# Four images' q*v products and Toeplitz products issued between the parts of the first image's front, and q*v in blocks of 128 tokens

## The chip, the cores and the metric

One core of a Trainium2 chip runs the whole program. The metric is the time of one execution on the device in microseconds; three executions of the kernel before are given. The core has a matrix engine (TensorE, PE in the profile, with PEld for its weight loads), a vector engine (VectorE, DVE), a scalar engine (ScalarE, ACT), GpSimd (POOL) and a sync engine (SyncE, SP), which in this kernel does little but issue DMAs. Each engine works through its own queue of instructions in order.

## The reference, cut to what matters

Eight images of 56 x 56 tokens with 192 channels pass through four layers, each added to its input and each preceded by a group norm: a gated Toeplitz layer, a shifted-window attention, a depthwise 3x3 convolution and a selective scan. The change concerns the first layer:

```
q, v, p = silu(gn(x) @ q_w.T + q_b), silu(... v_w ...), silu(... p_w ...)   # 192 -> 576 channels
qv = q * v
o1 = toeplitz(qv along w, a1)      # 576 channels, a 56 x 56 Toeplitz matrix per channel
o2 = toeplitz(qv along h, a2)
x  = x + (p * (o1 + o2)) @ o_w.T + o_b
```

The Toeplitz coefficients a1 and a2 come from a small network and a decay and are the same for all images. The other three layers follow image by image; the scan of layer 3 runs in four directions over 3136 tokens with 384 channels of 16 states each. All arithmetic is float32.

## The kernel before, in words

The program has five parts, in this order.

**Coefficients** (lines 145 to 184): both tables of Toeplitz coefficients are computed and put into DRAM (`ext`).

**q*v products** (lines 187 to 221): for each of the eight images, x is loaded on SP's queue, its group statistics are taken, and x is normalized. Then 28 blocks of TT = 112 tokens are multiplied with the 1152 columns of the q and v weights in three column groups of 384, each as two matmuls (lines 213 and 214, the two halves of the channels). ScalarE applies Silu (line 215), VectorE multiplies q with v (line 216), and the result is stored on SP's queue (line 218) to `qv_d`. A float32 matmul stands in the trace as two records, so 8 x 28 x 3 x 2 = 1344 matmuls are some 2688 records.

**Toeplitz products** (lines 224 to 277): for each of two axes, for each of six blocks of 96 channels (`c0`), both groups of four images are loaded as `tzx` (line 250, 16 DMAs on SP's queue, one for each image and half, 56 partitions each; along h the pieces in DRAM are 28 x 96 contiguous floats, along w they are 96 floats, 384 bytes). Within a block there are four groups of 24 channels: two DMAs on SP's queue (line 258) spread the coefficients of a group into one of three `tm` tiles of 112 x 24 x 112, as two diagonal 56 x 56 Toeplitz blocks, in runs of 224 bytes. Each channel and each group of four images is one 112 x 112 x 112 matmul (line 263). ScalarE and VectorE take turns (line 269) in copying four channels' result back into `tzx`, and 16 DMAs on GpSimd's queue (line 277) store the block. A `tm` load must wait until TensorE is done with the tile's previous contents, three groups earlier. A `tzx` load must wait for the store of the block that had the buffer before.

**Set-up and front of image 0**: constants, the attention's bias and masks (98 tiny DMAs on ScalarE's queue, line 339), the convolutions' diagonal matrices, and then `front(0)` (line 1133), which is the part of all four layers ahead of the scans: `gate` (416), `attention` (495), `conv2` (676), `inner` (757) and `steps` (833). They are generators that yield between pieces of work. Their instructions have line 76 in the trace for image 0, since they pass through a recorder (`Meter`) whose costs the later planner uses. `front(0)` is run to its end by `drain`, with nothing between its pieces.

**Scans** (from line 1137): a written order, with a planner that steps the front of the next image and the end of the last one into the gaps of the scans. The planner's costs come from the record of `front(0)`.

Outside the scans the framework places the instructions of each engine by its own schedule, with the program's order as priority; the order that comes out is known from the built program. The two Toeplitz steps and the front share the in-order queue of SP for their loads, and the pools of SBUF and PSUM decide what has to wait for what.

Of the kernel before, what the change touches and what calls it, by code (L numbers as in the profile page):

```python
# [15 lines left out]
F32 = mybir.dt.float32  # L16
AF = mybir.ActivationFunctionType
# [5 lines left out]
H = W = 56  # L23
# [58 lines left out]
def model(ctx: ExitStack, tc: tile.TileContext, a: dict, out: bass.AP):  # L82
# [5 lines left out]
    def load_const(pool, name, eng=None):  # L88
        t = pool.tile(list(a[name].shape), F32, name=name + "_sb")
        (eng or nc.sync).dma_start(out=t, in_=a[name])  # L90
        return t
# [24 lines left out]
    def blocks(ap):  # L116
        return ap.rearrange("(k p) l -> p k l", p=CP)

    def group_stats(x, sp, ps, mean_out, rstd_out):

        st = sp.tile([CP, 2, NCH, 6], F32, name="gn_st")
        mv = sp.tile([CP, 2, 2], F32, name="gn_mv")
        for k in range(2):
            for j in range(NCH):
                nc.vector.bn_stats(out=st[:, k, j, :], in_=x[:, k, j * CH : (j + 1) * CH])
            nc.vector.bn_aggr(out=mv[:, k, :], in_=st[:, k].rearrange("p j s -> p (j s)"))
        pm = ps.tile([128, 512], F32, name="ps_gn", tag="ps")
        nc.tensor.matmul(pm[:CP, 0:2], gmat, mv[:, :, 0], start=True, stop=True)
        nc.vector.tensor_copy(mean_out, pm[:CP, 0:2])

        dm = sp.tile([CP, 2], F32, name="gn_dm")
        nc.vector.tensor_sub(dm, mv[:, :, 0], mean_out)
        nc.vector.tensor_mul(dm, dm, dm)
        nc.vector.tensor_add(dm, dm, mv[:, :, 1])
        pv = ps.tile([128, 512], F32, name="ps_gn", tag="ps")
        nc.tensor.matmul(pv[:CP, 0:2], gmat, dm, start=True, stop=True)
        sd = sp.tile([CP, 2], F32, name="gn_sd")
        nc.scalar.activation(sd, pv[:CP, 0:2], AF.Sqrt, bias=eps5[:CP])
        nc.vector.reciprocal(rstd_out, sd)

    def normalize(dst, src, mean, rstd):
        nc.vector.tensor_scalar(dst, src, mean, rstd, ALU.subtract, ALU.mult)
# [41 lines left out]
            nc.gpsimd.dma_start(out=blocks(ext[i]), in_=ea)  # L184


    with (
        tc.tile_pool(name="qv_w", bufs=1) as wp,
        tc.tile_pool(name="qv", bufs=2) as sp,
        tc.tile_pool(name="qv_ps", bufs=2, space=PSUM) as ps,  # L190
        tc.tile_pool(name="qv_ps4", bufs=6, space=PSUM) as ps4,
    ):
        wqv = wp.tile([CP + 1, 2, 2 * D1], F32, name="wqv")
        nc.sync.dma_start(out=wqv[:CP, 0, :], in_=a["wqv"][0:CP])
        nc.sync.dma_start(out=wqv[:, 1, :], in_=a["wqv"][CP : 2 * CP + 1])
        for b in range(B):
            x = sp.tile([CP, 2, L], F32, name="x0")
            nc.sync.dma_start(out=x, in_=blocks(a["x"][b]))
            group_stats(x, sp, ps, stats0[:, b, :, 0], stats0[:, b, :, 1])
            xn = sp.tile([CP + 1, 2, L], F32, name="xn0")  # L200
            nc.gpsimd.memset(xn[CP : CP + 1, 1, :], 1.0)

            for k in range(2):
                normalize(xn[:CP, k, ::-1], x[:, k], stats0[:, b, k, 0:1], stats0[:, b, k, 1:2])
            for g in range(NCH):
                qv = sp.tile([TT, 4, D1], F32, name="qv")
                for t in range(4):
                    tok = slice((4 * g + t) * TT, (4 * g + t + 1) * TT)
                    sl = sp.tile([TT, 2 * D1], F32, name="sl", bufs=3)
                    for n in range(3):  # L210
                        pq = ps4.tile([TT, 384], F32, name="ps_qv")
                        col = slice(n * 384, (n + 1) * 384)
                        nc.tensor.matmul(pq, xn[:CP, 0, tok], wqv[:CP, 0, col], start=True, stop=False)
                        nc.tensor.matmul(pq, xn[:, 1, tok], wqv[:, 1, col], start=False, stop=True)
                        nc.scalar.activation(sl[:, col], pq, AF.Silu)
                    nc.vector.tensor_mul(qv[:, t, :], sl[:, :D1], sl[:, D1:])
                for c in range(D1 // CP):
                    nc.sync.dma_start(
                        out=qv_d[b][c, g * CH : (g + 1) * CH, :].rearrange("(t p) c -> p t c", p=TT),
                        in_=qv[:, :, c * CP : (c + 1) * CP],  # L220
                    )


    NB = min(4, B)
    TC = 24
    G = NB * (H // 2)
    with (
        tc.tile_pool(name="tz", bufs=4) as sp,
        tc.tile_pool(name="tz_t", bufs=1) as tp,
        tc.tile_pool(name="tz_ps", bufs=8, space=PSUM) as ps,  # L230
    ):

        tm = [tp.tile([TT, TC, TT], F32, name=f"tm{i}") for i in range(3)]
        for t in tm:
            nc.gpsimd.memset(t, 0.0)
        n_t = 0
        for ax in range(2):
            along_h = "(h u w) c -> u h w c"
            along_w = "(u h w) c -> u w h c"
            stored = "(w u h) c -> u w h c"  # L240
            size = dict(h=H, u=2) if ax == 0 else dict(w=W, u=2)
            for c0 in range(D1 // CP):
                xs = []
                for b0 in range(0, B, NB):
                    x = sp.tile([TT, G, CP], F32, name="tzx")
                    xs.append((b0, x))
                    for b in range(NB):
                        v = qv_d[b0 + b][c0].rearrange(along_w if ax else along_h, **size)
                        for u in range(2):
                            nc.sync.dma_start(out=x[u * W : (u + 1) * W, b * 28 : (b + 1) * 28, :], in_=v[u])  # L250
                for c1 in range(0, CP, TC):
                    t = tm[n_t % 3]
                    n_t += 1
                    e = ext[1 - ax][c0 * CP + c1 : c0 * CP + c1 + TC, :]

                    src = bass.AP(e.tensor, e.offset, [[1, W], [TT, TC], [1, W]])
                    for u in range(2):
                        nc.sync.dma_start(out=t[u * W : (u + 1) * W, :, u * W : (u + 1) * W], in_=src)
                    for b0, x in xs:
                        for c2 in range(0, TC, 4):  # L260
                            po = ps.tile([TT, 4, G], F32, name="ps_tz")
                            for c in range(4):
                                nc.tensor.matmul(  # L263
                                    po[:, c, :], t[:, c2 + c, :], x[:, :, c1 + c2 + c], start=True, stop=True
                                )
                            cs = slice(c1 + c2, c1 + c2 + 4)
                            copy = nc.vector.tensor_copy if (c2 // 4) % 2 else nc.scalar.copy

                            copy(  # L269
                                x[:, :, cs].rearrange("p (b g) c -> p b g c", b=NB)[:, :, ::-1, :],  # L270
                                po.rearrange("p c (b g) -> p b g c", b=NB),
                            )
                for b0, x in xs:
                    for b in range(NB):
                        v = o_d[ax][b0 + b][c0].rearrange(stored if ax else along_h, **size)
                        for u in range(2):
                            nc.gpsimd.dma_start(out=v[1 - u], in_=x[u * W : (u + 1) * W, b * 28 : (b + 1) * 28, :])  # L277


    with (  # L280
        tc.tile_pool(name="w", bufs=1) as wp,
        tc.tile_pool(name="sc", bufs=2) as sp,
        tc.tile_pool(name="bc", bufs=NP) as bcp,
    ):
        p_b, o_b, qkv_b, pr_b = (load_const(wp, n) for n in ("p_b", "o_b", "qkv_b", "pr_b"))
        cb2, cb3, dt_b = (load_const(wp, n) for n in ("cb2", "cb3", "dt_b"))
        ln_g, ln_b, w_out, w_dt = (load_const(wp, n) for n in ("ln_g", "ln_b", "w_out", "w_dt"))
# [5 lines left out]
        nc.vector.memset(ones, 1.0 / DI)  # L293
        zero2 = wp.tile([128, NG], F32, name="zero2")
        nc.vector.memset(zero2, 0.0)

        ysum = wp.tile([128, ND, L], F32, name="ysum")
        slab = wp.tile([128, SLAB], F32, name="slab")
        slab_f = wp.tile([128, SLAB_F], F32, name="slab_f")

# [651 lines left out]
        pairs = [(i, d, k) for i in range(len(chunks)) for d in range(ND) for k in range(NP)]  # L952
        bms, cms, deltas, dus, xcs, states, hss, das, hcs, yps, xds = ({} for _ in range(11))

        delta2 = wp.tile([128, 2, ND, CH + 2], F32, name="delta2")

        for u in range(2):
            nc.gpsimd.memset(delta2[:, u, :, 0 : CH + 2 : CH + 1], 1e30)

        def load_bc(i, k):  # L960
            b, slot, j = chunks[i]
            for ts, name, r0 in ((bms, "bm", 0), (cms, "cm", NS)):
# [166 lines left out]
                pass  # L1129


        with tc.tile_pool(name="ps0", bufs=8, space=PSUM) as ps:
            drain(front(0), costs.setdefault("front", []))
        psa = ctx.enter_context(tc.tile_pool(name="ps_a", bufs=2, space=PSUM))
        psy = ctx.enter_context(tc.tile_pool(name="ps_y", bufs=2, space=PSUM))
        ps = ctx.enter_context(tc.tile_pool(name="ps", bufs=2, space=PSUM))
# [196 lines left out]
```

## Time and profile before

| what | value |
|---|---|
| median of three executions | 22507.34 us (22483.73 to 22516.53) |
| the profiled execution | 22523.93 us |
| its span | 22522.1 us |
| TensorE busy | 18316.9 us (81%) |
| VectorE busy | 16557.5 us (74%) |
| GpSimd busy | 16170.0 us (72%) |
| ScalarE busy | 12501.5 us (56%) |
| first scan (line 1017) starts | 3738.0 us |

The page divides the span into 40 slices of 563 us each and gives the busy share of each engine in tenths. Line numbers are those of the kernel before. A group such as "L263 PE MATMUL ps_tz<-tzx,tm" is a line, an engine, an operation and the tiles that it writes and reads. What follows "idle before" or stands in square brackets is the time for which the engine stood still ahead of the instruction and what released it; "issue" means that the profile shows no releaser. SPq rows are DMAs being issued on SP; their second column is the time that the issuing took, with what it had to wait for in its queue.

### The profile page before, as it was taken

To read this page: it belongs to the slowest core of one execution; us is meant where nothing else is said; L and a number is where in the kernel's file an instruction comes from. 1 tells how busy PE (TensorE), PEld (TensorE's weight loads), DVE (VectorE), ACT (ScalarE), POOL (GpSimd) and SP (SyncE) were. 2 spreads that over 40 slices of the span, in tenths; PEclk is the share of its full clock that TensorE was granted. 3 is DMA by queue.
4 is the path that set the end of the run, shared out by engine and by line. 5 is a ranking of instruction groups with operands and counts; after the bars stand their busy time and mean duration, and the time that the engine had idled before them with its cause. 6 is when DMAs were issued, how large, how long until landed. Compare 5 with 4: busy or idle time off the path is not lost. (4 is left out here: it accounts for less than half of the span.)

```text
span 22522.1 us, 201129 instructions
## 1 busy us (share of the span) xinstructions
PE 18316.9 (81%) x58660; PEld 9648.2 (43%) x58660; DVE 16557.5 (74%) x13156; ACT 12501.5 (56%) x31864; POOL 16170.0 (72%) x8500
## 2 busy tenths in 40 slices
PE   8866677878897888888887888788978888887666
PEld 4566433434343344434443444344434444343233
DVE  3211113997699868997799779986898789967998
ACT  3311234665667566655666576746665666556555
POOL 0000003897789878887898778977898789878999
PEclk9988778989899999999999989998999999998888
DMA  3479215444553456445544455345534564445333
GB/s 90 106 197 187 74 47 160 140 131 147 176 155 124 135 172 176 122 128 166 180 132 127 156 183 148 120 141 179 167 118 133 163 187 130 123 149 179 129 129 110
DMA packets 2536340, 3220.45 MB, mean 143 GB/s; under 512 B 1045261, under 2 KB 2488687, under 8 KB 2504272
## 3 DMA queue, kind: packets, MB, share of 16 engines
q1 hardware_dynamic: 2515010, 3091.32, 46.2%
q0 software_dynamic: 15520, 116.14, 1.3%
q8 instruction: 465, 7.62, 0.1%
q14 instruction: 641, 5.25, 0.1%
q10 hardware_dynamic: 4704, 0.12, 0.0%
HBM read 2631.56 MB, written 575.48 MB: 142 GB/s over the span
## 5 line engine op out<-in xcount | busy, mean ns | idle before, releaser
L993 POOL TENSOR_TENSOR hs<-du,bm 128x896 f32<-128x896 f32 x5376 | 11140.7, 2107 | 87.2 <-DVE ps_a L1017 46.9
L1038 PE MATMUL ps_y<-hc,ident_sb 128*128 128x448 f32 x21504 | 9845.4, 592 | 742.9 <-POOL hc L1023 665.7
L1017 DVE TENSOR_TENSOR_SCAN ps_a<-ps_a,hs 128x898 f32<-128x898 f32 x3360 | 6796.3, 2023 | 1093.1 <-ACT ps_a L1008 895.4
L1008 ACT ACTIVATE ps_a<-delta,A_logs_sb 128x449 f32<-128x449 f32 x10752 | 6859.9, 638 | 355.0 <-DVE hs L1017 72.9
L1038 PEld LDWEIGHTS ps_y<-hc,ident_sb 128*128 128x128 f32 x21504 | 4290.3, 208 | 4809.5 <-issue 3546.5
L1023 POOL TENSOR_TENSOR hc<-hs,cm 128x896 f32<-128x896 f32 x2016 | 4077.0, 2022 | 2194.0 <-DVE hs L1017 1054.5
L1023 DVE TENSOR_TENSOR hc<-ps_a,cm 128x896 f32<-128x896 f32 x3360 | 3667.7, 1092 | 1207.7 <-PE ps_y L1038 921.5
L1017 DVE TENSOR_TENSOR_SCAN hs<-ps_a,hs 128x898 f32<-128x898 f32 x2016 | 4063.4, 2016 | 331.2 <-ACT ps_a L1008 253.6
L1030 ACT COPY state<-ps_a 128x2 f32<-128x2 f32 x3359 | 528.9, 157 | 3950.3 <-DVE hc L1023 3947.8
L981 POOL TENSOR_TENSOR du<-delta,xcd 128x448 f32<-128x448 f32 x672 | 719.6, 1071 | 1268.7 <-DMA xcd<-xc 1268.7
L263 PE MATMUL ps_tz<-tzx,tm 112*112 112x112 f32 x4608 | 889.5, 369 | 471.4 <-issue 272.2
L277 POOL DMA_DIRECT2D o<-tzx x192 | 97.9, 514 | 1498.7 <-DVE tzx L269 1018.6
L803 PE MATMUL ps_f<-slab 128*128 128x448 f32 x2646 | 1090.3, 548 | 60.1 <-DMA slab<-dg_d 48.0
L263 PEld LDWEIGHTS ps_tz<-tzx,tm 112*112 112x112 f32 x4608 | 884.0, 200 | 477.1 <-issue 476.0
L269 DVE COPY tzx<-ps_tz 112x448 f32<-112x448 f32 x288 | 179.9, 624 | 1180.3 <-PE ps_tz L263 910.5
L269 ACT COPY tzx<-ps_tz 112x448 f32<-112x448 f32 x288 | 153.3, 532 | 1206.0 <-PE ps_tz L263 975.2
L998 ACT COPY hs<-state 128x2 f32<-128x2 f32 x4608 | 817.5, 177 | 2.7 <-POOL hc L1023 2.5
L76 PE MATMUL ps_f<-slab 96*96 96x448 f32 (+6 forms) x2306 | 744.8, 519 | 87.7 <-DMA slab<-x 35.5
L633 PE MATMUL ps_f<-ident_sb,slab 98*98 98x98 f32 x1344 | 331.7, 315 | 586.2 <-ACT slab L626 586.2
L735 PE MATMUL ps_f<-slab 96*96 96x448 f32 x1764 | 725.5, 547 | 40.8 <-DVE slab L722 40.8
L803 PEld LDWEIGHTS ps_f<-slab 128*128 128x128 f32 x2646 | 507.7, 193 | 560.7 <-issue 502.5
L1030 ACT COPY state<-hs 128x2 f32<-128x2 f32 x2016 | 379.0, 188 | 581.5 <-DVE hs L1017 545.1
(215 smaller groups left out, 17752.8 us busy)
## 6 DMA issues: line engine op xcount, KB each, us to landing
bm<-bc SPq DMA_DIRECT2D x1792, 448.0 KB
cm<-bc SPq DMA_DIRECT2D x1792, 448.0 KB
xcd<-xc SPq DMA_DIRECT2D x840, 224.0 KB
dl<-slab SPq DMA_DIRECT2D x224, 672.0 KB
delta<-dl SPq DMA_DIRECT2D x224, 672.0 KB
tzx<-qv SPq DMA_DIRECT2D x192, 588.0 KB
o<-tzx POOLq DMA_DIRECT2D x192, 588.0 KB, 16.5
slab<-x SPq DMA_DIRECT2D x224, 336.0 KB
```

Source lines behind the costliest of these rows:

```text
L76: return f(*args, **kw)
L263: nc.tensor.matmul(po[:, c, :], t[:, c2 + c, :], x[:, :, c1 + c2 + c], start=True, stop=True)
L735: nc.tensor.matmul(p[:CP, :CH], dg[:, k, t, :], xp[:, u, k, dy : dy + 8, dx : dx + W], start=t == 0, stop=t == 8,)
L803: nc.tensor.matmul(p[:, :CH], dg[:, t, :], xp[:, 8 * j + dy : 8 * j + dy + 8, dx : dx + W], start=t == 0, stop=t == 8,)
L981: nc.gpsimd.tensor_mul(du[:, 0, :], deltas[i][:, d, 1 : CH + 1], xcs.pop((i, d)))
L993: nc.gpsimd.tensor_mul(hs[:, :, tokens(i)[0]], dus[i, d].to_broadcast([128, NG, CH]), bms[i, k])
L998: nc.scalar.copy(hss[g][:, :, tokens(i)[1]], src)
L1008: nc.scalar.activation(dA[:, n, :], deltas[i][:, d, at : at + CH + 1], AF.Exp, scale=negA[:, slot, d, c : c + 1])
L1017: nc.vector.tensor_tensor_scan(h, dA, hs, 0.0, ALU.mult, ALU.add)
L1023: (nc.gpsimd if on_pool(d, k) else nc.vector).tensor_mul(hc, h[:, :, tokens(i)[0]], cms[i, k])
L1030: nc.scalar.copy(states[i][:, d, NG * k : NG * k + NG], h[:, :, tokens(i)[2]])
L1038: nc.tensor.matmul(yps[i, d][:, :CH], ident, hcs[g][:, n, :], start=k + n == 0, stop=k + n == NP + NG - 2)
```

## The change

The two stages become generators, `products(images, beside)` and `toeplitz(images, beside)`, and are run twice. Images 0 to 3 go through both at once as before, ahead of everything else. Images 4 to 7 are stepped between the pieces of `front(0)`: after each piece, 0.55 of its recorded cost is added to an account, and the second run is advanced while the account is positive; a q*v block counts 4.3 and four channels of the Toeplitz product count 1.0. What is left over when `front(0)` has ended is issued then, ahead of the scans.

Further edits:

- q*v takes blocks of 128 tokens (six sets of four blocks and one block of 64 for each image) where it took 28 of 112.
- The Toeplitz stage handles four images at a time, so that the coefficients are spread into `tm` for each half of the images.
- `tzx` has three buffers of one image group in the first run (four, two for each channel block, before), two in the second. In the second run the products have three PSUM banks (six before), the Toeplitz stage four (eight before) and `front(0)` four (eight before), and VectorE alone copies the Toeplitz results.
- `ysum`, `delta2` and the scan's pools are made after the second run has ended, where they stood at the head of the set-up.

```diff
-        with tc.tile_pool(name="ps0", bufs=8, space=PSUM) as ps:
-            drain(front(0), costs.setdefault("front", []))
+        with tc.tile_pool(name="ps0", bufs=4 if later else 8, space=PSUM) as ps:
+            log = costs.setdefault("front", [])
+            first, others, spent = front(0), (us for stage in (products, toeplitz) for us in stage(later, True)), 0.0
+            while log_of(first, log) is not None:
+                spent += 0.55 * sum(cost for _, cost in log[-1])
+                while later and spent > 0.0:
+                    us = next(others, None)
+                    if us is None:
+                        break
+                    spent -= us
+            for _ in others if later else ():
+                pass
...
-        for b in range(B):
+            for b in images:
...
-            for g in range(NCH):
-                qv = sp.tile([TT, 4, D1], F32, name="qv")
-                for t in range(4):
-                    tok = slice((4 * g + t) * TT, (4 * g + t + 1) * TT)
+                for t0 in range(0, L, 512):
+                    n_t = min(4, (L - t0) // 64)
+                    p_t = (L - t0) // n_t if n_t < 4 else 128
+                    qv = sp.tile([128, 4, D1], F32, name="qv")
+                    for t in range(n_t):
+                        tok = slice(t0 + t * p_t, t0 + (t + 1) * p_t)
...
+                        yield 4.3
...
-                for b0 in range(0, B, NB):
-                    x = sp.tile([TT, G, CP], F32, name="tzx")
+                    x = sp.tile([TT, G, CP], F32, name="tzx", bufs=2 if beside else 3)
...
-                            copy = nc.vector.tensor_copy if (c2 // 4) % 2 else nc.scalar.copy
+                            copy = nc.vector.tensor_copy if (c2 // 4) % 2 or beside else nc.scalar.copy
...
+                            yield 1.0
...
+    now, later = range(min(4, B)), range(min(4, B), B)
+    for stage in (products, toeplitz):
+        for _ in stage(now, False):
+            pass
```

## The prediction

> **What bounds the kernel now.** The change touches only what lies ahead of the first scan, so I looked first at the page's slices (563 us each), which say where that is, and then asked for the busy time in stretches whose limits I set where the tiles change.
>
> ```profile
> PE   8866677878897888888887888788978888887666
> DVE  3211113997699868997799779986898789967998
> ACT  3311234665667566655666576746665666556555
> DMA  3479215444553456445544455345534564445333
> ```
>
> Up to the seventh slice VectorE, ScalarE and GpSimd are mostly idle; first TensorE, then the DMAs, then TensorE again lead. From 3738 us on it is the scans. The built programs' orders on all engines agree from there to the end, apart from the first few loads, so I carry the scans over unchanged at 22522.1 - 3738 = 18784 us.
>
> The stretches, with columns sum, PE, PEld, DVE, ACT, POOL busy, granted clock, DMA share, GB/s, are the q*v products, the Toeplitz stage's lead-in and two axes, and then set-up, gate, attention, conv2, inner and steps of image 0:
>
> ```profile
> 80.00:985.00 905.00, 884.94 (x2714) 479.69 (x2714) 252.94 (x382) 342.03 (x687) 16.24 (x6) 0.98 0.34 81
> 985.00:1017.00 32.00, 0.02 (x1) 0.05 (x1) 0.00 (x0) 0.00 (x0) 0.00 (x0) 0.52 0.84 195
> 1017.00:1693.00 676.00, 464.30 (x2405) 461.38 (x2406) 93.67 (x150) 79.83 (x150) 49.01 (x96) 0.82 0.79 200
> 1693.00:2374.00 681.00, 425.14 (x2205) 422.56 (x2203) 86.32 (x140) 73.45 (x138) 49.09 (x98) 0.80 0.82 175
> ...
> 2374.00:2487.00 113.00, 0.00 (x0) 0.00 (x0) 13.05 (x55) 1.84 (x3) 0.59 (x1) 0.50 0.21 58
> 2487.00:2700.00 213.00, 207.24 (x1075) 131.63 (x1076) 46.45 (x82) 50.27 (x61) 0.00 (x0) 0.95 0.41 95
> 2700.00:3122.00 422.00, 266.84 (x1274) 150.46 (x1272) 75.80 (x192) 196.23 (x763) 0.00 (x0) 0.60 0.06 12
> 3122.00:3236.00 114.00, 88.13 (x230) 38.48 (x231) 33.35 (x58) 5.25 (x9) 0.00 (x0) 0.87 0.24 66
> 3236.00:3560.00 324.00, 249.65 (x601) 120.99 (x599) 5.75 (x16) 79.78 (x103) 0.00 (x0) 0.85 0.30 102
> 3560.00:3738.00 178.00, 122.31 (x252) 51.46 (x252) 0.00 (x1) 91.25 (x118) 13.33 (x8) 0.62 0.68 232
> ```
>
> The q*v stage is TensorE-bound (885 of 905 us): 905 / 1344 = 0.673 us a product. The gate is too (207 of 213). In the Toeplitz stage TensorE works 65% of the time with the DMA engines at 0.8; in attention the gaps are short waits for the softmax; in steps the DMA leads.
>
> The order of time on SP shows the Toeplitz stage's limit, first along h, then along w, and what TensorE did meanwhile:
>
> ```profile
> 1140.88 30.66 SPq L250 DMA_DIRECT2D tzx<-qv  x16
> ...
> 1228.77 11.45 PE L263 MATMUL ps_tz<-tzx,tm 112*112 112x112 f32 x58 [34.98 <-DMA tm<-ext]
> ...
> 1815.55 87.03 SPq L250 DMA_DIRECT2D tzx<-qv  x16
> 1902.68 30.86 SPq L258 DMA_DIRECT2D tm<-ext  x8
> ```
>
> Along w a channel block costs SP's queue 87 us for sixteen loads in 384-byte runs and 31 for eight `tm` loads: 118, six times, which is the axis. Along h the loads take 31, but TensorE then waits 35 us for `tm` behind them. In work, TensorE does four channels in 1.54 us (the copies stand 1.54 us apart on alternating engines): 0.384 us a product, 192 products or 74 us a block.
>
> **What the Trainium skill says.** DMA: Bandwidth & Descriptors, under why a DMA increments its semaphore by 16, says that a DMA is spread over the largest number of engines up to 16 that divides its slowest dimension; 56 partitions give 14, an estimate of 0.875 for the share that SP's loads alone can reach. The 0.79 and 0.82 above, with GpSimd's stores in them, are near it. The same page, on issuing engines, says that queues share the 16 DMA engines, so stores on another queue are no free bandwidth. ScalarE: Activation LUTs, on what ACT_TABLE_LOAD costs, has about 1283 ns for a load plus about 1380 for a drain; this trace has 1283 a load (line 215), and shows no drain by itself.
>
> **The change part by part.**
>
> *q*v of images 0 to 3, in 128s.* A product costs by its 384 columns, not by its tokens, so 25 blocks instead of 28 are 150 products an image: 4 x 150 x 0.673 = 404 us. A 128-column weight load is hidden (PEld 480 under PE 885).
>
> *Toeplitz of images 0 to 3.* Half the images halve the `tzx` loads and products, but not the `tm` loads. Along w: 87 / 2 + 31 = 74 us a block. Along h: 15 + 31 = 46 on the queue, TensorE needs 37, and a third buffer lets the loads run ahead, but the DMA engines carry both queues' traffic; I take 55. With 32 lead-in and 17 for the last store: 32 + 6 x 55 + 6 x 74 + 17 = 823. The added `tm` traffic is 96 DMAs, 31 / 8 = 3.9 us each, 374 us of queue in the two runs together. This is the hidden price of the change.
>
> *Set-up*: 113 as before. The 98 table DMAs stand ahead of the second run's Silus on ScalarE, so hardly any of it is filled.
>
> *Second run.* In the built order, 37 of its 608 q*v matmuls (8 of them group statistics) come before the gate, 176 within it, 349 in attention, 46 in conv2; of the 1152 Toeplitz products 50 come in conv2, 494 in inner, 464 in steps and 144 after everything. Stage by stage:
>
> - Gate: TensorE has no room, so 176 x 0.673 = 118 on top of 213: 331.
> - Attention: 32 window groups; each has a gap of 4.6 us on TensorE between scores and transposes. 349 / 32 = 10.9 products are 7.3 us in it, 2.7 too long. Silu and Exp now alternate on ScalarE: 93 table loads before the first scan where there were 22, 71 x 1.28 = 91 us, about two a window group. One falls into the wait for the row maximum (1.29 us), the other between Exp and scaling, behind which the transposes and then TensorE's queue stand; some of it overlaps the products, and I charge 0.64. So 32 x 3.34 = 107, and 529. Bounds: TensorE's sum 267 + 235 = 502; with both loads and the page's drain on the chain, 32 x (2.7 + 5.3) = 256, 678.
> - conv2: 88 + 46 x 0.673 + 50 x 0.384 = 138 of TensorE; 150 with its waits (before: 114). Group statistics and normalizing of four images on VectorE, idle for most of the stretch, cost nothing; without that cover they would be some 10 us an image (252.94 / 8, less 28 multiplications at 0.758).
> - inner: 250 + 494 x 0.384 = 440 of TensorE; a quarter of the 74 us of gaps stays: 460. The Toeplitz copies on VectorE (0.62 in 1.54) are covered, since VectorE has 6 us of work here.
> - steps and what follows: now the queue. Axis w is 6 x 74 = 444, less about 40 loaded ahead (two buffers allow no more than a block), plus the stage's own DMA work 0.68 x 178 = 121, plus 40 for the last products, their store (16.5 us from issue to landing) and the first scan loads, which now stand behind the freed buffers and were hidden in steps before: 565, where steps took 178.
>
> Sum: 80 + 404 + 823 + 113 + 331 + 529 + 150 + 460 + 565 = 3455 us to the first scan, against 3738: 283 us less. The profiled execution was 22523.93 us, 17 above the median of those shown; the difference is taken off the median: 22507 - 283 = 22224.
>
> Four PSUM banks instead of eight for the front: a bank is held for about one product and one 0.6 us copy, and three or so are in use at once; 0, at worst a few us a stage.
>
> **The rivals.**
>
> *A, the forecast*: 22224.
>
> *B, the overlap is nearly complete.* Each stage at its floor: first Toeplitz run 780, attention 502, conv2 138, inner 440, steps and tail 500: 3288, 450 less, 22057. For it: VectorE and GpSimd are free, and the scheduler may load further ahead. Against: steps already has its DMA at 0.68.
>
> *C, SP's queue stalls the front; slower.* A `tm` load waits on SP for TensorE, and the front's next chunk load stands behind it, while TensorE's queue waits for that chunk. SP waited so for TensorE up to 23.8 us at a time (the queue's own waits: line 258 behind ps_tz, 215.6 us in 13 waits). The gain of 283 over 12 channel blocks is 23.6 us a block: from there on the kernel is slower. At 32 us a block: -283 + 384, so 22608. Against: in inner TensorE needs some 23 us for a group of 24 channels with the convolutions between, the queue 8 for its `tm`, so the loads should be early; in steps it is possible.
>
> *D, nothing is hidden.* The second run serially: 80 + 2 x (404 + 823) + 1364 = 3898, 160 more, 22667. It takes 160 us of hiding out of 1227 just to pay for the doubled `tm` loads; the forecast hides 443. The built order shows real interleaving, so I keep this low.
>
> **How the numbers follow.** A 0.64 (its own range 22100 to 22430), B 0.12, C 0.14, D 0.04, about even 0.06. A measurement of this kernel tells 0.2%, 45 us, from no change. Faster 0.76, same 0.06, slower 0.18. The range takes in B and most of C: 22050 to 22580.
>
> **What would show it.** Right: first scan near 3455; q*v of four images done by 485; first Toeplitz run over near 1310; attention about 530 long; steps and tail over 500 with TensorE waiting for DMA; `tm` loads doubled to 192; scans as long as before. Wrong: TensorE waits for slab loads (the front's) behind `tm` waits on SP (C); attention near 680 (drains); the first Toeplitz run near 1000, if its halved loads don't take half the time; or scans that differ in length, which would break the carry-over.

## The result, and the profile after

The changed kernel takes 22305.71 us (median of four executions, 22292.23 to 22327.07) against 22506.33 us (22483.73 to 22516.53) for the kernel before in the same comparison. The ratio is 0.9913, interval 0.9896 to 0.9930: 0.87% or about 200 us faster, some 80 us slower than the 22224 forecast and inside the range.

The profiled execution took 22327.07 us, its span is 22325.3 us, and the first scan (line 1015 now) starts at 3530.9 us where it started at 3738.0. That is 207 us earlier; from there to the end are 18794 us, against 18784 before, so the whole gain lies ahead of the first scan.

The page's slices of the kernel after, 558 us each, in tenths of busy time:

```profile
DVE  2122216997799768987899779976898789967998
ACT  2116114655666475756665566656565666556555
```

Ahead of the scans ScalarE reached 3 in no more than a few slices; now its fourth slice shows 6, which is attention with Silus of images 4 to 7 in it. In the seventh slice VectorE has 6 where it had 3: the scans begin earlier.

The stretches of the kernel after, limits again set where the tiles change. Columns as before: stretch, length, then PE, PEld, DVE, ACT and POOL busy with the number of records, granted TensorE clock, DMA share, GB/s. They are the q*v products of images 0 to 3, the Toeplitz lead-in and its two axes, then set-up, gate, attention, conv2, inner, and steps with everything up to the first scan:

```profile
74.00:491.00 417.00, 402.79 (x1212) 229.66 (x1211) 112.27 (x167) 152.82 (x307) 5.41 (x2) 0.97 0.32 81
491.00:524.00 33.00, 0.49 (x2) 0.52 (x3) 0.00 (x0) 0.00 (x0) 6.90 (x3) 0.50 0.87 175
524.00:850.00 326.00, 223.18 (x1152) 220.22 (x1150) 44.97 (x72) 38.30 (x72) 24.37 (x48) 0.80 0.88 204
850.00:1244.00 394.00, 223.07 (x1152) 220.78 (x1152) 44.98 (x72) 38.30 (x72) 24.32 (x48) 0.76 0.88 185
1244.00:1383.00 139.00, 23.28 (x60) 13.18 (x61) 31.38 (x89) 10.84 (x18) 5.95 (x3) 0.55 0.34 89
1383.00:1700.00 317.00, 316.92 (x1422) 192.31 (x1420) 86.12 (x146) 96.51 (x155) 2.71 (x1) 1.00 0.43 102
1700.00:2266.00 566.00, 505.70 (x1998) 286.43 (x1998) 137.25 (x279) 355.89 (x1008) 2.71 (x1) 0.80 0.18 42
2266.00:2387.00 121.00, 118.39 (x326) 55.46 (x325) 38.91 (x67) 17.44 (x33) 6.90 (x3) 0.97 0.63 147
2387.00:2968.00 581.00, 446.86 (x1747) 331.70 (x1745) 94.61 (x160) 81.66 (x104) 24.31 (x48) 0.88 0.65 177
2968.00:3531.00 563.00, 313.14 (x1404) 253.71 (x1404) 90.01 (x145) 94.83 (x121) 29.76 (x55) 0.71 0.79 196
```

The last three of these stretches are not those of the forecast. It counted 50 Toeplitz products of the second run into conv2, 494 into inner and 608 into what follows; in the stretches above there are 4, 572 and 576 (line 263's records, two a product). The 50th product ends at 2415.5 us, 10 us behind conv2's last convolution, and the 544th at 2911.5, with inner's last matmul. With these limits the last three stretches are:

```profile
2266.00:2415.50 149.50, 146.89 (x450) 77.89 (x448) 49.50 (x88) 19.03 (x35) 6.90 (x3) 0.98 0.62 144
2415.50:2911.50 496.00, 405.95 (x1562) 297.25 (x1561) 79.02 (x130) 67.85 (x92) 20.26 (x40) 0.90 0.62 171
2911.50:3531.00 619.50, 325.55 (x1469) 265.74 (x1467) 95.01 (x153) 107.06 (x131) 33.82 (x63) 0.70 0.81 201
```

Set against the sum of the prediction, with these three for the last rows (some 12 us of conv2's own matmuls, which the forecast had in inner, now count to conv2):

| stage | forecast, us | measured, us | difference |
|---|---|---|---|
| q*v of images 0 to 3, end of it | 484 | 491 | +7 |
| first Toeplitz run | 823 | 753 | -70 |
| set-up | 113 | 139 | +26 |
| gate | 331 | 317 | -14 |
| attention | 529 | 566 | +37 |
| conv2 | 150 | 150 | 0 |
| inner | 460 | 496 | +36 |
| steps, and up to the first scan | 565 | 619 | +54 |
| first scan | 3455 | 3531 | +76 |

The largest miss is what follows inner; attention, inner and set-up each took 26 to 37 us more than forecast, and the first Toeplitz run gives 70 us back. In inner TensorE stood still for 90 us where a quarter of 74 was expected. The waits of TensorE in the kernel after, from inner to the first scan, say for what (total, times, longest, in us):

```profile
PE ps_tz L263 <- DMA tm<-ext: 228.3, 8, 46.2
...
PE ps_tz L263 <- DMA bc<-slab: 67.0, 2, 34.5
```

Toeplitz products waited for their coefficients, 295 us with the row below it, which names a store of the front that came last by the profile. Of the first row 67 us lie in inner (up to 2911.5) and 161 behind it. The waits of SP's own queue in the same stretch show what the loads stood behind:

```profile
SPq L791 <- ACT slab L76: 109.0, 21, 15.7
SPq L877 <- ACT slab L76: 106.0, 10, 17.1
SPq L820 <- PE ps_f L76: 88.3, 3, 33.8
SPq L259 <- PE ps_tz L263: 68.2, 12, 22.2
```

Lines 791 and 877 are stores of image 0's chunks (`zr` and `dl`), which wait on SP until ScalarE has made them; line 820 is a reload whose buffer TensorE still reads. Only the last row is a `tm` load waiting for its own tile. SP's order of time in inner shows such a place, followed by what TensorE did:

```profile
2525.44 0.32 SPq L259 DMA_DIRECT2D tm<-ext  x1
2559.60 0.34 SPq L820 DMA_DIRECT2D slab<-zr  x1
2564.39 0.34 SPq L825 DMA_DIRECT2D xc<-slab  x1
2564.79 0.41 SPq L259 DMA_DIRECT2D tm<-ext  x1
2568.68 0.79 SPq L825 DMA_DIRECT2D z<-slab  x1
2569.52 9.51 SPq L768 DMA_DIRECT2D slab<-in_w_in_dram  x2
2579.08 6.35 SPq L771 DMA_DIRECT2D slab<-x  x1
2585.48 2.92 SPq L259 DMA_DIRECT2D tm<-ext  x1
```

```profile
2590.53 9.51 PE L263 MATMUL ps_tz<-tzx,tm 112*112 112x112 f32 x48 [26.35 <-DMA tm<-ext]
```

From 2525 to 2559 nothing at all was issued on SP. The two halves of a `tm` tile went out at 2565 and 2585, after the front's reload, two stores and three loads, and TensorE's queue, with the front's own matmuls behind the Toeplitz product, stood still for 26 us until 2590.

The longest stop, 46 us, is at the change of axis, right behind inner's last matmul (SP, then TensorE):

```profile
2887.73 1.31 SPq L251 DMA_DIRECT2D tzx<-qv  x1
2911.64 0.34 SPq L820 DMA_DIRECT2D slab<-zr  x1
...
2921.02 38.11 SPq L251 DMA_DIRECT2D tzx<-qv  x7
```

```profile
2970.07 9.50 PE L263 MATMUL ps_tz<-tzx,tm 112*112 112x112 f32 x48 [46.16 <-DMA tm<-ext]
```

One of the eight loads of the first block along w went out at 2888. The other seven stood behind the reload of `zr` until TensorE had ended inner, and then behind two stores, and took 38 us from 2921 on: nothing of this block had been hidden.

### The profile page after: what moved, and what is told of

It reads as the page before. It is cut to its first block, busy times and chain, and to the rows that moved or that the text cites. A ratio compares the mean times of both kernels' runs of the same rounds, so it can differ in the third digit from the quotient of the medians.

```text
span 22325.3 us, 200421 instructions
## 1 busy us (share of the span) xinstructions
PE 18177.3 (81%) x58372; PEld 9602.0 (43%) x58372; DVE 16627.2 (74%) x13276; ACT 12465.2 (56%) x31719; POOL 16168.9 (72%) x8503
## 5 line engine op out<-in xcount | busy, mean ns | idle before, releaser
L269 DVE COPY tzx<-ps_tz 112x448 f32<-112x448 f32 x432 | 269.9, 625 | 1551.8 <-PE ps_tz L263 1420.2
L76 PE MATMUL ps_f<-slab 96*96 96x448 f32 (+6 forms) x2306 | 694.8, 480 | 25.9 <-DMA slab<-dg_d 22.7
L621 ACT ACTIVATE slab<-slab,mxs 98x98 f32<-98x98 f32 x1344 | 489.5, 365 | 370.9 <-DVE mxs L618 370.9
```

The costliest lines, as they stand in the source:

```text
L76: return f(*args, **kw)
```

## The experiments

All were compared with the kernel before on the same chip; ratios are to that. Where two of them are set against each other, I subtract ratios; 0.1% is 22.5 us.

| kernel | ratio | interval | first scan, us |
|---|---|---|---|
| after | 0.9913 | 0.9896 to 0.9930 | 3530.9 |
| e1 before, q*v in 128s alone | 0.9957 | 0.9943 to 0.9971 | 3640.9 |
| e2 after, both halves ahead, serially | 1.0034 | 1.0021 to 1.0047 | 3832.6 |
| e7 only q*v beside the front | 0.9962 | 0.9947 to 0.9977 | 3657.7 |
| e3 only Toeplitz beside the front | 0.9907 | 0.9892 to 0.9921 | 3537.5 |
| e4 second run's loads on GpSimd's queue | 1.0007 | 0.9998 to 1.0015 | 3727.4 |
| e6 front's stores on GpSimd's queue | 0.9864 | 0.9849 to 0.9879 | 3415.4 |
| e5 before, front with four banks | 1.0014 | 1.0007 to 1.0021 | 3766.3 |
| e8 after, front with five banks | 0.9946 | 0.9929 to 0.9962 | 3633.4 |
| e9 e6, tables on GpSimd's queue, early start | 0.9856 | 0.9841 to 0.9870 | 3389.8 |
| e10 e6, pace 0.70 | 0.9868 | 0.9854 to 0.9883 | 3430.4 |
| e11 e9 and e10 together | 0.9852 | 0.9837 to 0.9867 | 3383.7 |
| e12 after, no Silu in the second run | 0.9842 | 0.9825 to 0.9858 | 3367.2 |

### e1: blocks of 128 tokens alone

Edit to the kernel before:

```diff
-            for g in range(NCH):
...
-                    tok = slice((4 * g + t) * TT, (4 * g + t + 1) * TT)
+            for t0 in range(0, L, 512):
+                n_t = min(4, (L - t0) // 64)
+                p_t = (L - t0) // n_t if n_t < 4 else 128
...
+                    tok = slice(t0 + t * p_t, t0 + (t + 1) * p_t)
```

> The kernel before with q*v in blocks of 128 tokens and nothing else changed. Forecast (a product costs by its 384 columns): 8 x 18 products fewer at 0.673 us, 97 us less, 22410. Rival (the stage is bound by ScalarE's Silus or by the work per token): no change, 22507.

0.43%, or about 97 us at the ratio, and 97 us at the first scan. That is what 144 products fewer cost at 0.673 us, so a product costs by its columns here, as the prediction had it. This piece alone is about half of what the whole change gains.

### e2: both halves ahead of the front, serially

```diff
-    for stage in (products, toeplitz):
-        for _ in stage(now, False):
-            pass
+    for images in (now, later):
+        for stage in (products, toeplitz):
+            for _ in stage(images, False):
+                pass
...
-        with tc.tile_pool(name="ps0", bufs=4 if later else 8, space=PSUM) as ps:
+        with tc.tile_pool(name="ps0", bufs=8, space=PSUM) as ps:
...
-            first, others, spent = front(0), (us for stage in (products, toeplitz) for us in stage(later, True)), 0.0
+            first, others, spent = front(0), iter(()), 0.0
```

> The changed kernel with both halves of the images ahead of the set-up, nothing beside the front. This prices what the halving costs when nothing is hidden. With the prediction's sum for a Toeplitz run (823): first scan at 3898, 160 later than in the kernel before, 22667. With the 752 us that the changed kernel's first Toeplitz run took: 74 + 2 x (417 + 752) + 1364 = 3776, 38 later, 22545. If halving costs the same as half the old stage (1389 / 2 each): 97 less than before, 22410.

The first scan is 95 us later than before. That is rival D, whose price had been put at 160: slower all the same. A second half takes some 1220 us here (1240 to 2460), of which the changed kernel hides 3832.6 - 3530.9 = 302; the prediction meant to hide 443 of 1227. So the two errors are separate: the halves are 65 us cheaper than forecast, and 141 us less of the second is hidden.

### e7 and e3: which of the two is hidden

e7 keeps only the q*v products beside the front and runs the second Toeplitz run after it; e3 computes all q*v ahead and keeps only the Toeplitz run beside the front.

```diff
-            first, others, spent = front(0), (us for stage in (products, toeplitz) for us in stage(later, True)), 0.0
+            first, others, spent = front(0), products(later, True), 0.0
...
+        for _ in toeplitz(later, True):
+            pass
```

```diff
-    for stage in (products, toeplitz):
-        for _ in stage(now, False):
+    for stage, images in ((products, range(B)), (toeplitz, now)):
+        for _ in stage(images, False):
...
-            first, others, spent = front(0), (us for stage in (products, toeplitz) for us in stage(later, True)), 0.0
+            first, others, spent = front(0), toeplitz(later, True), 0.0
```

> Only the q*v products of images 4 to 7 between the front's pieces; their Toeplitz run after the front, ahead of the scans. With both halves ahead it was 22597, with both beside 22306, with Toeplitz alone beside 22309. If the hiding adds up, q*v alone hides almost nothing: 22590. If the two take each other's gaps, q*v alone hides what the stages of the changed kernel show, 417 of q*v for 317 + 566 + 121 - 749 = 255 of longer stages, 162: 22435, or some 50 more if the Toeplitz run with two buffers is slower or the scans' first loads stand bare behind it.

> The q*v products of all eight images ahead, only the Toeplitz products of images 4 to 7 between the front's pieces; they then fall into the gate (480 products) and attention (576) instead of inner and steps. If the second q*v run is hidden little (TensorE is full in the gate, and in attention its products run slowly) and the Toeplitz run hides better where the DMA engines are idle: first scan near 74 + 834 + 752 + 139 + 415 + 530 + 114 + 324 + 198 = 3380, 150 before the changed kernel's 3531, 22155. If the hiding of q*v is what gains, and a Toeplitz run costs 641 us wherever it stands: near 3690, 22465.

Against e2, moving q*v alone gains 0.72% (162 us), Toeplitz alone 1.27% (286 us), and both together only 1.21% (272 us). They don't add up: alone, each stands mainly in gate and attention; together, the Toeplitz run is pushed back into inner and steps. e7 came out near its second figure (162 us hidden), which had assumed that the two take each other's gaps. For e3 none of the figures expected came out; it is as fast as the whole change. Its stretches of gate and attention show why it is not faster:

```profile
1795.00:2250.00 455.00, 393.76 (x2045) 317.58 (x2045) 123.74 (x204) 47.89 (x54) 20.28 (x40) 0.91 0.77 178
2250.00:2885.00 635.00, 472.70 (x2417) 361.33 (x2416) 164.27 (x337) 199.82 (x772) 24.47 (x50) 0.73 0.57 114
```

The Toeplitz products turn the gate from 213 us into 455 and attention from 422 into 635, at a clock of 0.73 and with TensorE idle for 162 us of it. The largest wait of TensorE in that attention is for the softmax again, in e3 (total, times, longest):

```profile
PE ps_f L76 <- ACT slab L76: 130.9, 46, 5.0
```

In the kernel before this wait was 152.9 us. The Toeplitz products came between rows of windows and not into those gaps, so they were added to attention's time rather than hidden in it.

### e4 and e6: what shares SP's queue

e4 takes the second run's loads off SP's queue, e6 the front's stores and the `zr` reload of image 0.

```diff
-                            nc.sync.dma_start(out=t[u * W : (u + 1) * W, :, u * W : (u + 1) * W], in_=src)
+                            (nc.gpsimd if beside else nc.sync).dma_start(out=t[u * W : (u + 1) * W, :, u * W : (u + 1) * W], in_=src)
```

```diff
-                            nc.sync.dma_start(out=zr_d[b][:, d, j * CH : (j + 1) * CH], in_=zt[:, j % 2, :])
+                            (nc.sync if b else nc.gpsimd).dma_start(out=zr_d[b][:, d, j * CH : (j + 1) * CH], in_=zt[:, j % 2, :])
...
-                    nc.sync.dma_start(out=dl_d[2 * o + s][b][:, :, tok], in_=dl[:, s])
+                    (nc.sync if b else nc.gpsimd).dma_start(out=dl_d[2 * o + s][b][:, :, tok], in_=dl[:, s])
```

> The changed kernel with the second Toeplitz run's loads (tzx and tm) issued on GpSimd's queue instead of SP's. If SP's in-order queue couples the front and the Toeplitz loads (TensorE waited 295 us for tm and for bc behind which tm stood, from inner on), some 100 to 200 of it goes: 22110 to 22210. If the transfers themselves are the limit: 22306, unchanged. If GpSimd prepares small pieces slowly: slower, above 22400.

> The changed kernel with image 0's stores of inner and steps (zr, xc, z, bc, dl) and the reload of zr on GpSimd's queue, so that SP's queue no longer stands still for ScalarE or TensorE ahead of Toeplitz loads. If that standing still (109 us behind ScalarE's zr, 88 for the reload of zr, 106 for dl) is what makes tm late: TensorE's waits for tm (67 us in inner, 161 after it) shrink and 60 to 150 us go, 22155 to 22245. If the transfers or the PSUM banks are the limit: 22306, unchanged.

e4 gave up the whole gain of the change (0.94% or 212 us slower than it). It does not take the loads out from behind waiting stores: GpSimd's queue carries the stores of the Toeplitz blocks, which wait for VectorE's copies (352 us in 11 waits from inner to the first scan in e4), and the loads of the next block now stand behind them, as in this part of GpSimd's order of time:

```profile
2790.94 1.10 POOL L251 DMA_DIRECT2D tzx<-qv  x2
2827.85 4.03 POOL L277 DMA_DIRECT2D o<-tzx  x8 [35.81 <-DVE tzx L269]
2833.36 0.51 POOL L251 DMA_DIRECT2D tzx<-qv  x1 [1.48 <-DMA o<-tzx]
```

The price of issuing changed too, and the two were not separated. So e4 does not tell the theories apart; these loads are better left on SP as long as those stores are on GpSimd.

e6 does. It is 0.49% or 110 us faster than the change. Up to inner's last matmul, and from there to the first scan, e6 has:

```profile
2368.00:2880.90 512.90, 447.06 (x1683) 323.46 (x1682) 89.48 (x152) 68.50 (x94) 36.51 (x69) 0.92 0.72 183
2880.90:3415.00 534.10, 342.79 (x1469) 273.84 (x1467) 94.94 (x152) 106.76 (x131) 64.02 (x108) 0.73 0.87 223
```

and the change, with as many records in the first of the two (for the second see 2911.50 to 3531.00 above):

```profile
2387.00:2911.50 524.50, 434.45 (x1684) 319.68 (x1683) 89.61 (x152) 69.43 (x94) 20.26 (x40) 0.90 0.62 169
```

The waits of TensorE in e6, in both together:

```profile
PE ps_f L76 <- ACT slab L76: 87.2, 19, 16.9
...
PE ps_tz L263 <- DMA tm<-ext: 69.0, 7, 25.8
```

Inner is only 12 us shorter, what follows it 85. The first products along w follow inner without a stop, where there had been one of 46 us, and the blocks along w come 81 us apart instead of 94. The wait for `tm` fell from 228 us (295 with the row that named the store) to 69. In inner it fell from 67 to 16, but waits for the front's own loads of x (19 us) and for ScalarE (12) came in its place, and SP now stood still 158 us for TensorE ahead of those loads (line 771; 22 in the change). In all, the wait for ScalarE is 87 us, 12 in the change. The remaining 18 us at the first scan lie ahead of inner, where the edit changes nothing; the change's profiled execution was the slowest of its four.

The loads, their sizes and the tiles are the same; only the stores and the reload ahead of them on SP's queue were taken away. In the change these DMAs waited 353 us there for ScalarE and TensorE (lines 791, 820, 825, 833, 858, 877), and their issuing took 64. At the change of axis it is the waiting that counts, since only 1 us was issued between 2889 and 2921; in steps, where most of the 64 us lie, the share of the two was not separated. The Trainium skill (DMA: Bandwidth & Descriptors, under "Issuing engines are not separate DMA queues") has it that issuing on several engines saves only the sequencer's time to start a DMA, usually small. Here the sequencer was held up by waits as well, and separating DMAs that wait for compute from loads that don't was worth some 110 us. Whether the transfers share the 16 engines, as the same section says, no run here tests.

### e5 and e8: PSUM banks

```diff
-        with tc.tile_pool(name="ps0", bufs=8, space=PSUM) as ps:
+        with tc.tile_pool(name="ps0", bufs=4, space=PSUM) as ps:
```

```diff
-            tc.tile_pool(name="qv_ps4", bufs=3 if beside else 6, space=PSUM) as ps4,
+            tc.tile_pool(name="qv_ps4", bufs=2 if beside else 6, space=PSUM) as ps4,
...
-            tc.tile_pool(name="tz_ps", bufs=4 if beside else 8, space=PSUM) as ps,
+            tc.tile_pool(name="tz_ps", bufs=3 if beside else 8, space=PSUM) as ps,
...
-        with tc.tile_pool(name="ps0", bufs=4 if later else 8, space=PSUM) as ps:
+        with tc.tile_pool(name="ps0", bufs=5 if later else 8, space=PSUM) as ps:
```

> The kernel before with four PSUM banks for the front of image 0 instead of eight, and nothing else changed. The prediction put this at 0, a few us a stage at worst: 22507 to 22520. Rival, from the run with Toeplitz products alone beside: its steps, with nothing beside them, took 14.9 us a chunk against some 10.7 in the kernel before; if the banks do that, 14 x 4.2 = 59 more, 22566 or above.

> The changed kernel with five PSUM banks for image 0's front, and two instead of three for q*v, three instead of four for Toeplitz in the second run. If the front's banks cost time here too: some 20 to 60 us less, 22245 to 22285. If the second run hides it, or needs its own banks: 22306 or more.

e5, which is the kernel before with four banks for the front, is 0.14% (32 us) slower, with 28 us at the first scan, between the two figures expected. Most of it is lost in steps. TensorE's waits there (from 3560 us to the first scan), first in the kernel before, then in e5:

```profile
PE ps_f L76 <- ACT slab L76: 32.8, 20, 6.0
```

```profile
PE ps_f L76 <- ACT slab L76: 73.6, 39, 7.4
```

Twice as many waits for ScalarE to empty a bank. Giving the front one of the others' banks doesn't pay: e8 is 0.33% or 74 us slower than the change, with attention at 684 us. TensorE's wait for Silu grew from 59.0 us to the following (e8, attention), with two q*v banks and with 90 table loads where the change has 67, two effects that e8 does not separate:

```profile
PE ps_qv L216 <- ACT sl L218: 103.2, 39, 3.8
```

### e12: the second run without Silu

```diff
-                            nc.scalar.activation(sl[:p_t, col], pq[:p_t], AF.Silu)
+                            nc.scalar.activation(sl[:p_t, col], pq[:p_t], AF.Copy if beside else AF.Silu)
```

> The changed kernel with a plain copy in place of Silu in the q*v products of images 4 to 7, which leaves their Silu out, so that ScalarE changes no table sets for them: 68 table loads fewer. If the table loads are what made attention 566 us where 529 was forecast (and 502 is TensorE's sum): attention near 530 and the kernel some 30 to 60 less, 22245 to 22275. If TensorE's slower products there are the limit: 22306, unchanged.

0.71% or 160 us faster than the change: far more than expected. Attention is 157 us shorter; at the first scan it is 164, since what lies ahead of attention took 25 less and what follows it 18 more. The groups of attention in the change (from 1690 us, which takes in 10 us of the gate), with busy time, mean ns of one, and the idle time before them with its releaser:

```profile
L76 PE MATMUL ps_f<-slab 98*32 98x98 f32 (+4 forms) x1092 | 197.7, 391 | 0.7 <-ACT slab L76 0.7
L216 PE MATMUL ps_qv<-wqv,xn 96*128 96x384 f32 (+1 forms) x352 | 174.3, 581 | 59.0 <-ACT sl L218 59.0
...
L218 ACT ACT_TABLE_LOAD x36 | 46.2, 1283 | 0.6
```

The same in e12, and below it e12's stretch:

```profile
L76 PE MATMUL ps_f<-slab 98*32 98x98 f32 (+4 forms) x1094 | 153.2, 322 | 0.0
L216 PE MATMUL ps_qv<-wqv,xn 96*128 96x384 f32 (+1 forms) x336 | 140.0, 498 | 1.1 <-ACT sl L218 1.1
```

```profile
1675.00:2084.00 409.00, 403.15 (x2001) 234.06 (x2000) 134.74 (x288) 268.00 (x947) 2.71 (x1) 0.98 0.25 61
```

The activation costs the same in both (0.49 us; the copy 488 ns, the Silu 491), so what is gone is the switching of tables. It cost TensorE more than its waits: 59 us of waits, and some 100 us of work, 506 us busy against 403 for the same 2000 records, at a granted clock of 0.80 against 0.98. How a switch reaches TensorE can be read off ScalarE's and TensorE's order of time at the end of one window's softmax in the change (a part of each):

```profile
2113.77 1.28 ACT L76 ACT_TABLE_LOAD   x1
...
2117.35 1.28 ACT L218 ACT_TABLE_LOAD   x1
2118.64 0.49 ACT L218 ACTIVATE sl<-ps_qv 128x384 f32<-128x384 f32 x1
```

```profile
2119.18 0.91 PE L216 MATMUL ps_qv<-wqv,xn 96*128 96x384 f32 x2 [2.08 <-ACT sl L218]
```

ScalarE loads Exp's table, works six exponentials, loads Silu's, and only at 2118.64 reads a q*v bank. TensorE meanwhile has filled the three banks and stands still for 2 us; the front's next transposes lie behind that product in its queue. The next matmuls then take about twice the time (line 217's pair: 0.81 us ahead of this stop, 1.54 after it). A longer stop shows the same: after 58 us of standing still in set-up, the first pairs of the second run took 1.49 to 1.65 us each, and 0.81 from 1369.7 on. The drain in the prediction's upper bound doesn't appear: Silu starts 0.01 us after the load's end. The Trainium skill (TensorE: Matmul & The Clock Gate, under "A second HAM failure mode: psum-queue depth-cycling") describes a bf16 kernel whose short idle spells between PSUM banks made the clock swing. This trace agrees with it for float32: 31 waits, none over 3.1 us, and a mean clock of 0.80. That the waits lower the clock is read from their order in time and from both going together; no run varied the one without the other.

### e9, e10, e11: filling set-up, and another pace

e9 is e6 with the 98 table DMAs moved from ScalarE's queue to GpSimd's and with 80 us in the account at the start; e10 is e6 with 0.70 in place of 0.55; e11 has all of it.

```diff
-                    nc.scalar.dma_start(
+                    nc.gpsimd.dma_start(
...
-            first, others, spent = front(0), (us for stage in (products, toeplitz) for us in stage(later, True)), 0.0
+            first, others, spent = front(0), (us for stage in (products, toeplitz) for us in stage(later, True)), 80.0
...
-                spent += 0.55 * sum(cost for _, cost in log[-1])
+                spent += 0.7 * sum(cost for _, cost in log[-1])
```

> The run with image 0's stores on GpSimd (0.9864 of the kernel before), and further the 98 table DMAs of the set-up on GpSimd's queue instead of ScalarE's and the account of the second run started at 80. In the changed kernel ScalarE issued these DMAs for 97 us while q*v's Silus stood behind them. If that is what leaves TensorE idle in the set-up: 132 q*v matmuls stand ahead of the gate instead of 37, 95 x 0.673 = 64 less, and no Toeplitz products are left at the end: 60 to 120 less, 0.981 to 0.984 of before. If x or the group statistics are what q*v waits for: 0.986.

> The run with image 0's stores on GpSimd, and 0.70 of the front's cost added to the account instead of 0.55: q*v ends in attention, 432 Toeplitz products stand in conv2 (50 before), 96 in steps (464) and none at the end (144). If steps and tail are long because the Toeplitz loads crowd there with the front's own DMAs: 50 to 100 less, 0.982 to 0.984 of before. If the Toeplitz loads take their time wherever they stand: 0.986.

> Both: table DMAs on GpSimd, account from 80, pace 0.70, image 0's stores on GpSimd. All q*v is done by the middle of attention, 312 Toeplitz products stand in attention and none in steps. If the two add: 0.978 to 0.981 of before. If Toeplitz products in attention hide as badly as in the run with Toeplitz alone (attention 635 us): 0.984 to 0.987.

In the change, ScalarE's order of time in set-up has this:

```profile
1256.83 96.90 ACTq L342 DMA_DIRECT2D slab<-in_table_dram  x97
1353.76 1.28 ACT L138 ACT_TABLE_LOAD   x1 [97.75 <-DMA slab<-in_table_dram]
```

The square root of the group statistics, and with it every Silu, stands 97 us behind those DMAs. In e9 the first second-run product starts at 1296.6 us instead of 1360.4, and from 1310 on TensorE is busy throughout. Yet of these 64 us only 26 arrive at the first scan, and the ratio is not distinguishable from e6's: less came than the 60 to 120 us expected. e10 and e11 came out at their second figures. The faster pace does nothing by itself: attention grows to 670 us in e10, since it then holds more of the second run. Between the placements of e6, e9, e10 and e11 no difference is clear of the intervals. The shortest is e11 with 0.9852, whose interval overlaps e6's and lies clear of the change's. It is faster than both kernels: 22160.18 us, some 0.6% below the change and 1.5% below the kernel before.

## Why the prediction was right, and where its terms were not

**Sign, range and carry-over: right.** The change is faster, 22305.71 lies within 22050 to 22580 and within A's own 22100 to 22430, and the scans are 10 us longer than carried over. That the sum came within 82 us is in part luck: it was 146 us too low elsewhere, and the first Toeplitz run, forecast 70 too high, took half of that back.

**q*v in 128s: right.** 97 us expected of the stage as a whole, 97 at the first scan in e1.

**First Toeplitz run: 70 too high.** Along h the 55 us a block held (326 us for six are 54.3). Along w the term was half of 87 us plus 31, 74; a block took 394 / 6 = 65.7 with the last store, and on SP 27 for the eight `tzx` loads and 35 for the `tm` loads, 62. Halving the loads more than halved the time that their issuing took (87 us for sixteen, 27 for eight); why isn't shown. D's price of 160 was too high by about as much: it was 95 in e2, whose second half took 1220 us where 1227 was forecast.

**Gate and conv2: 14 and 0 under the forecast**, TensorE-bound as expected (317 of 317 us, 147 of 149.5).

**Set-up: 139, not 113.** The step "98 table DMAs stand ahead of the second run's Silus" was right; that set-up would last "as before" was not. The 97 DMAs took 97 us, the first q*v product started at 1360 behind them, and the 37 q*v matmuls that the built order puts ahead of the gate, which the sum priced at nothing, took 28 us from there to the gate's first matmul at 1388. e9 does not shorten set-up (the gate starts at 1385): it fills it with more products, and that 26 us arrive is a chance agreement with the 26 here.

**Attention: the size was near (566 for 529) by luck, the working wrong in two terms that nearly cancelled.** Products were charged 2.7 us a window group for what doesn't fit the gap, 86 us in all; without the switches they cost less than nothing, since attention took 409 us with them in e12 and 422 without them before. The switches were charged 0.64 us a window group, 20 in all; they cost (566 - 409) / 32 = 4.9, 157 in all. The step that failed is the path: Silu's load does stand between Exp and scaling, but what waits for it is not the transposes; it is the q*v product ahead of them in TensorE's queue, which needs one of three banks, and the matmuls after it run slower. And 502, "TensorE's sum", was no floor: its 267 us had been measured at a clock of 0.60.

**Inner: 460 forecast, 496 measured.** The step that failed is "a quarter of the 74 us of gaps stays": TensorE stood still for 90 us, 67 of them for `tm`, and part of it was made good because TensorE's work was 406 us and not 440. The only reason that the prediction gives for early loads is rival C's counter-argument: the queue needs 8 us for a `tm` pair and has 23. It has them only if nothing on the queue waits. C had the coupling in one direction, `tm` waiting for TensorE and holding up the front's loads; what ran is mostly the other one, the front's stores waiting for ScalarE and TensorE and holding up `tm`. The 110 us that e6 gains are 9 us for each of 12 blocks, below C's break-even of 23.6, so C's sign did not come. In inner itself e6 gains only 12 us; what would fill its gaps stays open.

**Steps and tail: 565 forecast, 619 measured; the largest miss.** The price of a block was right: 444 + 121 for six blocks is 94 us each, and they came 94 to 95 apart. The step that failed is "less about 40 loaded ahead". The first block's loads stood behind the `zr` reload and two stores on SP, TensorE waited 46 us for the block, and nothing was gained. The last products, their store and the scan's first loads took 54 us where 40 were forecast. In e6, with that reload and the stores on another queue, the first block had no such wait.

**Four banks for the front, "0, at worst a few us a stage": wrong,** 32 us in the kernel before (e5), most of it in steps, where TensorE waits for ScalarE to empty a bank. In the change part of it lies under the second run's products; how much isn't settled.

**What stays open.** A second run whose Silu needs no switch, by computing it from Exp's table, was not tried; e3 kept q*v out of attention, but put Toeplitz products there. As an estimate it can gain at most about what e12 does.

## What to carry to other kernels

Before filling gaps of a stage with other work, list what the work shares with it besides the engine that idles: an in-order DMA queue with waits in it, PSUM banks that a third engine empties, a function table. Take stores that wait for compute off the queue that feeds loads, and don't move the loads behind other such stores; and price a table switch by who waits for the bank it delays, not by the load's own duration. A sum of busy times is a floor only at the clock at which it was measured: ask for the clock of each stretch along with it.

## What the runs showed of the hardware that I had not expected

- Waits of TensorE of at most 3.1 us, 31 of them in 566 us, went with a granted clock of 0.80; without them it was 0.98, and the same matmuls took 403 us where they had taken 506. Filling attention's gaps without switches made it shorter (409 us) than it was with its gaps empty (422, clock 0.60).
- Without 68 table loads of 1.283 us, 87 us by themselves on an engine that was not the busiest, the kernel was 160 us faster (e12).
- The second run's `tzx` and `tm` loads on GpSimd's queue, behind stores that waited 352 us for VectorE, made the kernel 212 us slower than on SP's (e4). The front's stores taken off SP's queue made it 110 us faster (e6).
